# Loading, normalising and convolving in a two-layer selective-scan kernel: larger pieces of x, xn by two engines, block 3 of the convolution split between TensorE and VectorE

## The chip, the cores and the metric

The kernel runs on one core of a Trainium2 chip. The metric is device time in microseconds (us) for one launch. A difference is given against the median of several runs of the kernel before. TensorE (PE) multiplies matrices, VectorE (DVE) and ScalarE (ACT) work element by element, GpSimd (POOL) does so too, and SyncE (SP) issues most DMAs. Each engine has one queue and takes its instructions in order.

## The reference

An image of 64 x 64 positions with 96 channels passes two layers with the same skeleton. Cut to what matters here:

```python
x = x + layer0(_gn(x)); x = x + layer1(_gn(x))   # _gn: 32 groups of 3 channels, mean and variance over the image

def layer(x):                     # x: (1, 64, 64, 96), D_INNER = 192
    xz = x @ in_proj_w            # 96 -> 2 * 192
    x_val, z = split(xz)
    x_val = silu(depthwise_conv_3x3(x_val) + conv_b)
    y = sum of four selective scans of x_val over the 4096 positions
    y = layernorm(y) * silu(z)
    return y @ out_proj_w         # 192 -> 96
```

## The kernel before

Everything is fp32 and channel-major: `xT` holds 96 channels on 96 partitions by 4096 positions. The 192 inner channels are three blocks of 64, called b or T = 0, 1, 2. A block's tile has 128 partitions: the lower 64 hold the even pieces of 512 positions, the upper 64 the odd pieces, so that a tile has 4 chunks (NCH = 4) of 512 columns (HT = 512), and a chunk covers 1,024 positions.

The work runs in these stages:

- **Load** (L151 to L163). x is read in eight pieces g of 512 positions, each by one DMA, alternately from SP's and ACT's queue, into tiles `xt` with four buffers. TensorE transposes each piece in four parts into PSUM (`pt`), and VectorE copies `pt` to `xT` (L163). After that, VectorE takes the group statistics (`bn_stats`, L1268), and one DMA writes all of `xT` to a DRAM tensor `xs` (L1269), from which the end of the layer reads it again.
- **Head of a layer** (`head`, L1044 to L1180). `bn_aggr` and two small matmuls with the averaging matrix `gav` (L1064, L1070) give the group mean `gm` and, through ACT's Ln and Exp (L1071, L1072), the reciprocal deviation `rs`. VectorE normalises `xT` to `xn` in eight pieces (L1077). TensorE projects `xn` into each block: `project(b, c)`, copied by ACT into a padded image `pad[b]` (L1088), and `borders(b)`, the rows above and below each piece (L1102, copied at L1106). The depthwise 3x3 convolution then runs on two engines at once. Blocks 0 and 1 are done by VectorE in `conv(b, s)`, for two chunks at a time: one multiply (L1158) and eight multiply-adds (L1160). Block 2 is done by TensorE in `conv_by_products(2, c)`: nine matmuls per chunk with diagonal matrices `diag` that ACT makes (L1172). `finish` adds bias and Silu on ACT (L1127), giving `u`, and ACT starts `y` (L1042). Last, `gate(b, c)`, twelve times: TensorE projects `z` (L1114), ACT takes Silu into one of three buffers `sz` (L1119), and a DMA on SP's queue writes it to DRAM (L1120).
- **Scans.** Layer 0 goes through `near_scans`, which needs all of `u` and starts with matmuls `nu<-u,wide` (L276). Layer 1 goes through `scans`, a long loop whose order is pinned by hand once it has begun; it starts with a load of ACT's function table (L84) and the projections `pj<-u,xw`.
- **Tail** (`tail`): layer norm, gate, output projection, the sum with x, and for layer 0 the `bn_stats` of the next layer (L1243).

Outside the pinned loop, a planner orders each engine's queue: it goes through the instructions by priority (the order of the program text) as its own model thinks them ready, hands out buffers, and sets the waits. An instruction further down in the text can therefore stand earlier in a queue. For example, the DMA of `ipw` (L1274) stands in SP's queue at 2.21 us, before the DMA of `xs` (L1269) at 15.91 us.

The block order in the head before is:

```python
conv(0, 0)
for c in range(NCH):
    conv_by_products(2, c)
for b, s in ((1, 0), (0, 1), (1, 1)):
    conv(b, s)
```

Of the kernel before, what the change touches and what calls it, by code (L numbers as in the profile page):

```python
# [8 lines left out]
F32 = mybir.dt.float32  # L9
BF16 = mybir.dt.bfloat16  # L10
AF = mybir.ActivationFunctionType
ALU = mybir.AluOpType
# [4 lines left out]
HW = 64  # L17
L = HW * HW
DM = 96
# [5 lines left out]
HT = TC // 2  # L25
NCH = L // TC
SR = HT // HW
# [16 lines left out]
def two_ss2d_layers(  # L44
# [29 lines left out]
    nc = tc.nc  # L74

    const = ctx.enter_context(tc.tile_pool(name="const", bufs=1))
    pers = ctx.enter_context(tc.tile_pool(name="pers", bufs=1))
# [13 lines left out]
    ident = const.tile([128, 128], F32, name="ident")  # L91
# [25 lines left out]
    eps5 = const.tile([128, 1], F32, name="eps5")  # L117
    nc.vector.memset(eps5, 1e-5)
    gav = const.tile([DM, DM], F32, name="gav")
    nc.sync.dma_start(out=gav, in_=gavg)  # L120

# [23 lines left out]
    xs = dpool.tile([DM, L], F32, name="xs")  # L147
# [2 lines left out]

    xp = ExitStack()  # L151
    xT = xp.enter_context(tc.tile_pool(name="xT0", bufs=1)).tile([DM, L], F32, name="xT0")
    with tc.tile_pool(name="ld", bufs=4) as ld, tc.tile_pool(
        name="ldp", bufs=4, space=PSUM
    ) as ldp:
        xr = x.rearrange("(g j p) c -> g p j c", p=128, j=4)
        for g in range(8):
            xt = ld.tile([128, 4, DM], F32, tag="xt", name=f"xt{g}")
            (nc.sync if g % 2 == 0 else nc.scalar).dma_start(out=xt, in_=xr[g])
            pt = ldp.tile([DM, 512], F32, tag="pt", name=f"pt{g}")  # L160
            for j in range(4):
                nc.tensor.transpose(pt[:, j * 128 : (j + 1) * 128], xt[:, j, :], ident)
            nc.vector.tensor_copy(xT[:, g * 512 : (g + 1) * 512], pt)  # L163

    def columns(t, h, cols):

# [874 lines left out]
    def start_y(mul, ds, T, s=slice(0, L // 2)):  # L1041
        mul(y[T][:, s], u[T][:, s], ds[:, T : T + 1])  # L1042

    def head(l, xT, w):  # L1044

        ipw_s, v, ds = w["ipw"], w["v"], w["ds"]
        with ExitStack() as sc:
            cv = sc.enter_context(tc.tile_pool(name=f"cv{l}", bufs=1))
            cw = sc.enter_context(tc.tile_pool(name=f"cw{l}", bufs=3))
# [7 lines left out]
                nc.gpsimd.memset(t[HALF[1], NCH - 1, SR + 1, 1 : HW + 1], 0.0)  # L1057


            gst = cv.tile([DM, 6], F32, name=f"gst{l}")  # L1060
            gm, rs = gst[:, 2:3], gst[:, 5:6]
            nc.vector.bn_aggr(gst[:, 0:2], w["st"].rearrange("p a b -> p (a b)"))
            pm = cvp.tile([DM, 1], F32, tag="z", name=f"pm{l}", bufs=3)
            nc.tensor.matmul(pm, gav, gst[:, 0:1], start=True, stop=True)  # L1064
# [6 lines left out]
            nc.scalar.activation(rs, pv, AF.Ln, bias=eps5[0:DM])  # L1071
            nc.scalar.activation(rs, rs, AF.Exp, scale=-0.5)  # L1072

            xn = cv.tile([DM, L], F32, name=f"xn{l}")
            for g in range(8):
                s = slice(g * 512, (g + 1) * 512)
                nc.vector.tensor_scalar(xn[:, s], xT[:, s], gm, rs, ALU.subtract, ALU.mult)  # L1077
            xr = xn.rearrange("p (r w) -> p r w", w=HW)

            def project(b, c):  # L1080
# [43 lines left out]
            W2 = HW + 2  # L1124

            def finish(b, cut, of):
                nc.scalar.activation(  # L1127
                    u[b][:, cut].rearrange("p (c r w) -> p c r w", r=SR, w=HW), of, AF.Silu,
                    bias=v[:, b, V_CB : V_CB + 1],
                )  # L1130
                start_y(nc.scalar.mul, ds, b, cut)

            def conv_by_products(b, c):

                ps = cvp.tile([128, HT], F32, tag="in", name=f"cp{l}_{b}_{c}", bufs=3)
                for k, (i, j) in enumerate(taps):
                    nc.tensor.matmul(  # L1137
                        ps.rearrange("p (r w) -> p r w", w=HW), diag[:, k, :],
                        pad[b][:, c, i : i + SR, j : j + HW],
                        start=(k == 0), stop=(k == len(taps) - 1),  # L1140
                    )
                finish(
                    b, slice(HT * c, HT * (c + 1)), ps.rearrange("p (c r w) -> p c r w", c=1, w=HW)
                )

            def conv(b, s):


                room = cw.tile([128, 2, SR, W2], F32, tag="acc", name=f"acc{l}_{b}_{s}")
                acc = room.rearrange("p c r w -> p c (r w)")[:, :, 0 : SR * W2 - 2]  # L1150
                for k, (i, j) in enumerate(taps):
                    o = i * W2 + j
                    src = pad[b].rearrange("p c r w -> p c (r w)")[
                        :, 2 * s : 2 * s + 2, o : o + SR * W2 - 2
                    ]
                    wk = v[:, b, V_CW + k : V_CW + k + 1]
                    if k == 0:
                        nc.vector.tensor_scalar_mul(acc, src, wk)  # L1158
                    else:
                        nc.vector.scalar_tensor_tensor(acc, src, wk, acc, ALU.mult, ALU.add)  # L1160
                finish(b, slice(1024 * s, 1024 * (s + 1)), room[:, :, :, 0:HW])

            for b in (0, 1, 2):
                project(b, 0)
# [5 lines left out]
            diag = cv.tile([128, len(taps), 128], F32, name=f"diag{l}")  # L1170
            for k in range(len(taps)):
                nc.scalar.mul(diag[:, k, :], ident, v[:, 2, V_CW + k : V_CW + k + 1])  # L1172
            conv(0, 0)
            for c in range(NCH):
                conv_by_products(2, c)
            for b, s in ((1, 0), (0, 1), (1, 1)):
                conv(b, s)
            for b in range(3):
                for c in range(NCH):
                    gate(b, c)  # L1180
# [82 lines left out]
                    if 0 <= i - lag < NCH:  # L1263
                        step(order[i - lag])

    st = [pers.tile([DM, 8, 6], F32, name=f"st{l}") for l in range(2)]
    for g in range(8):
        nc.vector.bn_stats(st[0][:, g, :], xT[:, g * 512 : (g + 1) * 512])  # L1268
    nc.sync.dma_start(out=xs, in_=xT)  # L1269
    for l in range(2):  # L1270

        w = {"st": st[l], "next": st[1]}
        ipw_s = w["ipw"] = wts.tile([DM, 2 * DI], F32, name=f"ipw{l}")
        nc.sync.dma_start(out=ipw_s, in_=ipw[l])  # L1274
        v = w["v"] = wts.tile([128, 3, NV], F32, name=f"v{l}")
        op = w["op"] = wts.tile([128, 3, DM], F32, name=f"op{l}")
        for half in HALF:
            nc.sync.dma_start(out=v[half], in_=vec[l].rearrange("(b p) n -> p b n", b=3))
        for half in HALF:
            nc.sync.dma_start(out=op[half], in_=opw[l].rearrange("(b p) n -> p b n", b=3))  # L1280
        ds = w["ds"] = wts.tile([128, 3], F32, name=f"ds{l}")
        nc.vector.reduce_sum(ds, v[:, :, V_D : V_D + 4], axis=AX.X)
        sw = scan_weights(l)

        head(l, xT, w)
        xp.close()
        if l:
            scans(sw)
        else:
            covered = near_scans(sw)  # L1290
            with tc.If(covered < 1):
                for T in range(3):
                    start_y(nc.scalar.mul, ds, T)
                far_scans(sw)
        xp = ExitStack()
        xT = xp.enter_context(tc.tile_pool(name=f"xT{l + 1}", bufs=1)).tile(
            [DM, L], F32, name=f"xT{l + 1}"
        )
        tail(l, w, xT)
# [80 lines left out]
```

## Time and profile before

| what | us |
|---|---|
| median of 3 runs (1557.27 to 1559.94) | 1559.88 |
| the profiled execution | 1555.25 |
| its span, first to last instruction | 1553.5 |
| layer 0: start to first `bn_aggr` | 20.07 |
| layer 0: first `xn` to first VectorE convolution instruction | 22.89 to 31.17 |
| layer 0: convolution on VectorE | 31.17 to 73.8 |
| layer 0: convolution on TensorE | 42.19 to 73.4 |
| layer 0: first `sz` to first matmul of `near_scans` | 74.42 to 88.33 |
| layer 1: first `xn` to first VectorE convolution instruction | 224.67 to 233.61 |
| layer 1: convolution on VectorE | 233.61 to 276.24 |
| layer 1: first `sz` to table load of `scans` | 276.85 to 288.93 |

Over the whole span VectorE is busy for 87%, TensorE for 81%, ACT for 77% and GpSimd for 70%; these are means over all stages. In the profile's notation, "out<-in" names the tile written and the tiles read, and a bracket at the end of a timeline row gives the idle time before it and what released it. An fp32 matmul is carried out as two records in the trace, so `x144` matmuls of `cp` are 72 calls, 36 in each layer.

### The profile page before, as it was taken

How to read it: one execution, taken by the hardware profiler on the slowest of the kernel's cores; microseconds unless marked ns; L12 is line 12 of the kernel's file. 1: busy time of each engine (PE TensorE's matmuls, PEld its weight loads, DVE VectorE, ACT ScalarE, POOL GpSimd, SP SyncE). 2: the span in 40 equal slices, each digit the busy share in tenths (PEclk: the TensorE clock that was granted, in tenths of full speed). 3: DMA queues.
4: the chain of work that ended last, by engine and by line, in shares of the span. 5: the costliest groups of instructions: out<-in, count | busy, mean ns of one | idle time of the engine just before them, and what ended most of it. 6: DMA issues, size and time to landing. Idle time of an engine off the chain costs nothing.

```text
span 1553.5 us, 17352 instructions
## 1 busy us (share of the span) xinstructions
PE 1256.0 (81%) x5158; PEld 504.4 (32%) x5158; DVE 1350.1 (87%) x932; ACT 1203.1 (77%) x2476; POOL 1093.8 (70%) x577
## 2 busy tenths in 40 slices
PE   5954779769888979887888889797978888876778
PEld 3433424223233323332333333333333332322223
DVE  6836489339999999999999999999999999999976
ACT  3445134759999898989999999999898989987733
POOL 0032000019898989899998989898989999998750
PEclk8975689759999999999989999999999899999999
DMA  4031320432626263544526262526263443626233
GB/s 110 20 107 35 105 71 1 134 73 55 138 57 136 64 145 80 123 100 92 134 68 151 59 138 56 136 57 149 68 138 82 110 110 82 136 62 152 60 93 83
DMA packets 83059, 146.33 MB, mean 94 GB/s; under 512 B 31580, under 2 KB 33820, under 8 KB 82860
## 3 DMA queue, kind: packets, MB, share of 16 engines
q1 hardware_dynamic: 80844, 144.35, 38.4%
q10 hardware_dynamic: 2112, 0.79, 0.2%
q8 instruction: 42, 0.69, 0.2%
q14 instruction: 61, 0.50, 0.1%
HBM read 80.85 MB, written 12.13 MB: 60 GB/s over the span
## 4 chain that ended last, share of the span: by engine, by line
DVE 28%; issue 22%; PE 13%; ACT 10%; POOL 5%; DMA 5%; SPq 4%; DVEq 0%; POOLq 0%; ACTq 0%
DVE h L670 18%; DVE b L670 7%; POOL hc L670 4%; SPq L670 4%; ACT a L670 3%; PE ys L670 3%; DMA cb<-C 3%; PE b L670 2%; PE cp L1137 2%; ACT bT L670 2%; PE pj L670 2%; PE pd L670 1%; DVE w L670 1%; PE in L1084 1%; PE m L1205 1%
## 5 line engine op out<-in xcount | busy, mean ns | idle before, releaser
L670 POOL TENSOR_TENSOR hc<-h,cb 128x1024 f32<-128x1024 f32 x384 | 902.8, 2368 | 204.1 <-DMA dt<-sp 95.5
L670 DVE TENSOR_TENSOR_SCAN h<-a,carry,b 128x1024 f32<-128x1024 f32 x288 | 665.1, 2337 | 27.0 <-PE b L670 5.6
L670 ACT ACTIVATE a<-dt,am 128x1024 f32<-128x1024 f32 x384 | 438.6, 1143 | 92.3 <-DVE h L670 90.6
L670 PE MATMUL ys<-hc,fold 128*64 128x512 f32 x1536 | 429.4, 639 | 3.5 <-POOL hc L670 3.5
L670 ACT ACTIVATE bT<-duT,BT 128x192 f32<-128x192 f32 x1024 | 391.6, 445 | 5.1 <-PE b L670 3.0
L670 PE MATMUL b<-ident,bT 128*128 128x128 f32 x1536 | 222.0, 287 | 33.8 <-DVE h L670 27.6
L670 DVE TENSOR_TENSOR b<-b,du 128x1024 f32<-128x1024 f32 x192 | 232.0, 1208 | 3.5 <-PE b L670 3.2
L670 DVE TENSOR_TENSOR_SCAN h<-a,b 128x1024 f32<-128x1024 f32 x96 | 216.0, 2277 | 20.2 <-PE b L670 12.9
L670 PEld LDWEIGHTS b<-ident,bT 128*128 128x128 f32 x1536 | 174.2, 146 | 158.7 <-DVE h L670 99.7
L670 PE MATMUL b<-B,selh 96*128 96x512 bf16 x384 | 122.2, 401 | 96.1 <-DVE h L670 95.4
L670 PEld LDWEIGHTS ys<-hc,fold 128*64 128x64 f32 x1536 | 78.5, 139 | 140.8 <-issue 97.5
L670 PE MATMUL pd<-xd,dwb 29*64 29x512 f32 x192 | 60.3, 693 | 53.7 <-DVE w L670 46.9
L670 PEld LDWEIGHTS <-selh 96*128 96x128 bf16 x384 | 26.1, 98 | 222.5 <-DVE h L670 126.8
L670 PE MATMUL pj<-u,xw 64*124 64x512 f32 x192 | 94.2, 636 | 2.4 <-ACT sz L1119 1.7
L1160 DVE SCALAR_TENSOR_TENSOR acc<-pad,v,acc 128x1052 f32<-128x1052 f32 x64 | 79.6, 1308 | 0.2
L670 POOL TENSOR_TENSOR ln<-ln,w 128x512 f32<-128x512 f32 x45 | 57.6, 1279 | 14.8 <-DVE w L670 14.8
L670 PE MATMUL ys<-y,ident 128*128 128x512 f32 (+1 forms) x120 | 63.3, 634 | 0.0
L1137 PE MATMUL cp<-pad,diag 128*128 128x512 f32 x144 | 62.3, 593 | 0.0
L670 ACT CAST B<-pj 96x512 bf16<-96x512 f32 (+2 forms) x96 | 55.1, 575 | 6.4 <-PE pj L670 6.3
L670 POOL TENSOR_TENSOR sp<-sp,ln 128x512 f32<-128x512 f32 x45 | 57.5, 1278 | 0.0
L670 DVE SCALAR_TENSOR_TENSOR w<-pd,w 128x512 f32<-128x512 f32 x48 | 32.1, 668 | 29.2 <-ACT pd L670 28.6
L670 POOL TENSOR_TENSOR su<-sp,u 128x512 f32<-128x512 f32 x45 | 57.3, 1274 | 0.0
(164 smaller groups left out, 1142.2 us busy)
## 6 DMA issues: line engine op xcount, KB each, us to landing
cb<-C SPq DMA_DIRECT2D x256, 256.0 KB, 4.1
dt<-sp SPq DMA_DIRECT2D x192, 128.0 KB, 4.3
du<-su SPq DMA_DIRECT2D x192, 128.0 KB, 3.9
szd<-sz SPq DMA_DIRECT2D x24, 256.0 KB, 3.1
szt<-szd SPq DMA_DIRECT2D x24, 256.0 KB, 6.5
xT<-xs SPq DMA_DIRECT2D x8, 384.0 KB
xs<-xT SPq DMA_DIRECT2D x1, 1536.0 KB
xs<-xT SPq DMA_DIRECT2D x8, 192.0 KB, 2.3
```

The costliest lines, as they stand in the source:

```text
L670: ins = op(*args, **more)
L1084: nc.tensor.matmul(ps[half], ipw_s[:, 64 * b : 64 * b + 64], xn[:, g * 512 : (g + 1) * 512], start=True, stop=True,)
L1137: nc.tensor.matmul(ps.rearrange("p (r w) -> p r w", w=HW), diag[:, k, :], pad[b][:, c, i : i + SR, j : j + HW], start=(k == 0), stop=(k == ...
L1160: nc.vector.scalar_tensor_tensor(acc, src, wk, acc, ALU.mult, ALU.add)
L1205: nc.tensor.matmul(pm, pos, y[T][:, cut], start=(T == 0), stop=(T == 2))
```

## The change

The change has four parts.

1. x is read with four consecutive positions on each partition (1,536 consecutive bytes) in place of four rows of 384 bytes that lie 128 positions apart. There are eight buffers, all eight DMAs stand ahead of the transposes, and ACT in place of VectorE copies `pt` to `xT`, writing every fourth column. `bn_stats` reads `pt` in PSUM rather than `xT`.
2. The DMA of `xs` now directly follows the load, and the DMA of `gav` follows that of `xs`; before, `gav` was the first DMA of all.
3. The eight pieces of `xn` are split: VectorE does the even ones, ACT the odd ones, as `Identity(rs * x + shift)`, with a new small VectorE instruction for `shift = -gm * rs`.
4. `conv` takes any slice of chunks. Chunk 3 of block 2 moves from TensorE to VectorE, behind the other VectorE convolutions.

```diff
-    nc.sync.dma_start(out=gav, in_=gavg)
...
+    st = [pers.tile([DM, 8, 6], F32, name=f"st{l}") for l in range(2)]
-    with tc.tile_pool(name="ld", bufs=4) as ld, tc.tile_pool(
+    with tc.tile_pool(name="ld", bufs=8) as ld, tc.tile_pool(
         name="ldp", bufs=4, space=PSUM
     ) as ldp:
-        xr = x.rearrange("(g j p) c -> g p j c", p=128, j=4)
+        xr = x.rearrange("(g p j) c -> g p j c", p=128, j=4)
+        xts = [ld.tile([128, 4, DM], F32, tag="xt", name=f"xt{g}") for g in range(8)]
         for g in range(8):
-            xt = ld.tile([128, 4, DM], F32, tag="xt", name=f"xt{g}")
-            (nc.sync if g % 2 == 0 else nc.scalar).dma_start(out=xt, in_=xr[g])
-            pt = ldp.tile([DM, 512], F32, tag="pt", name=f"pt{g}")
+            (nc.sync if g % 2 == 0 else nc.scalar).dma_start(out=xts[g], in_=xr[g])
+        for g in range(8):
+            pt = ldp.tile([DM, 4, 128], F32, tag="pt", name=f"pt{g}")
             for j in range(4):
-                nc.tensor.transpose(pt[:, j * 128 : (j + 1) * 128], xt[:, j, :], ident)
-            nc.vector.tensor_copy(xT[:, g * 512 : (g + 1) * 512], pt)
+                nc.tensor.transpose(pt[:, j], xts[g][:, j, :], ident)
+            nc.scalar.copy(
+                xT[:, g * 512 : (g + 1) * 512].rearrange("c (p j) -> c j p", j=4), pt
+            )
+            nc.vector.bn_stats(st[0][:, g, :], pt.rearrange("c j p -> c (j p)"))
+    nc.sync.dma_start(out=xs, in_=xT)
+    nc.sync.dma_start(out=gav, in_=gavg)
...
+            nc.vector.scalar_tensor_tensor(shift, gm, -1.0, rs, ALU.mult, ALU.mult)
             xn = cv.tile([DM, L], F32, name=f"xn{l}")
             for g in range(8):
                 s = slice(g * 512, (g + 1) * 512)
-                nc.vector.tensor_scalar(xn[:, s], xT[:, s], gm, rs, ALU.subtract, ALU.mult)
+                if g % 2 == 0:
+                    nc.vector.tensor_scalar(xn[:, s], xT[:, s], gm, rs, ALU.subtract, ALU.mult)
+                else:
+                    nc.scalar.activation(xn[:, s], xT[:, s], AF.Identity, bias=shift, scale=rs)
...
             def conv(b, s):
-                room = cw.tile([128, 2, SR, W2], F32, tag="acc", name=f"acc{l}_{b}_{s}")
+                n = s.stop - s.start
+                room = cw.tile([128, 2, SR, W2], F32, tag="acc", name=f"acc{l}_{b}_{s.start}")
+                room = room[:, 0:n]
...
-                        :, 2 * s : 2 * s + 2, o : o + SR * W2 - 2
+                        :, s, o : o + SR * W2 - 2
...
-                finish(b, slice(1024 * s, 1024 * (s + 1)), room[:, :, :, 0:HW])
+                finish(b, slice(HT * s.start, HT * s.stop), room[:, :, :, 0:HW])
...
-            conv(0, 0)
-            for c in range(NCH):
+            conv(0, slice(0, 2))
+            for c in range(NCH - 1):
                 conv_by_products(2, c)
-            for b, s in ((1, 0), (0, 1), (1, 1)):
-                conv(b, s)
+            for b, c in ((1, 0), (0, 2), (1, 2)):
+                conv(b, slice(c, c + 2))
+            conv(2, slice(NCH - 1, NCH))
...
-    st = [pers.tile([DM, 8, 6], F32, name=f"st{l}") for l in range(2)]
-    for g in range(8):
-        nc.vector.bn_stats(st[0][:, g, :], xT[:, g * 512 : (g + 1) * 512])
-    nc.sync.dma_start(out=xs, in_=xT)
```

More of the change, by code (lines that the diff above doesn't have):

```diff
@@ L1057, in head @@
                 nc.gpsimd.memset(t[HALF[1], NCH - 1, SR + 1, 1 : HW + 1], 0.0)
-            gst = cv.tile([DM, 6], F32, name=f"gst{l}")
-            gm, rs = gst[:, 2:3], gst[:, 5:6]
+            gst = cv.tile([DM, 7], F32, name=f"gst{l}")
+            gm, rs, shift = gst[:, 2:3], gst[:, 5:6], gst[:, 6:7]
             nc.vector.bn_aggr(gst[:, 0:2], w["st"].rearrange("p a b -> p (a b)"))
```

## The prediction

> **What bounds the kernel now.** I read the page, then the chain of waits from 0 to 330 us, then the timeline of the three stretches that the change touches: the load (0 to 23 us) and the heads of layer 0 (23 to 88 us) and layer 1 (222 to 289 us). The rest, some 1,380 us of scans and tails, has no edited line; I take it as a constant that starts earlier or later. The chain's groups by line, in that window, put the convolution on TensorE first:
>
> ```profile
> by line: PE cp L1137 9.4%; PE in L1084 4.5%; issue 3.8%; PE pj L670 3.1%; PE m L1205 2.2%; DMA szd<-sz 1.5%; DVE g L1226 1.3%; ACT bT L670 1.2%; ACT sz L1119 1.2%; DVE y L1207 1.1%; DVE g L1223 0.9%; PE pd L670 0.9%; ACT diag L1172 0.8%; DV
> ...
> 244.71 31.10 PE cp L1137 x72
> ...
> 282.10 2.46 DMA szd<-sz
> ```
>
> So in a head the chain goes through the 72 records of `cp`, then the gates. The timeline of the load and of layer 0's head, and VectorE's of layer 1:
>
> ```profile
> 6.55 0.17 DVE L1282 TENSOR_REDUCE ds<-v 128x3 f32<-128x12 f32 x1 [3.60 <-DMA v<-in_vec_dram]
> ...
> 11.62 3.53 PE L162 MATMUL pt<-ident,xt 128*96 128x128 f32 x16 [3.48 <-DMA xt<-in_x_dram]
> ...
> 15.80 4.24 DVE L1268 BATCH_NORM_STATS2 st<-xT 96x6 f32<-96x512 f32 x7
> ...
> 20.07 0.37 DVE L1062 BATCH_NORM_AGGREGATE gst<-st 96x2 f32<-96x48 f32 x1
> ...
> 71.12 2.67 DVE L1160 SCALAR_TENSOR_TENSOR acc<-pad,v,acc 128x1052 f32<-128x1052 f32 x2
> ...
> 73.29 5.47 PE L1114 MATMUL z<-xn,ipw 96*64 96x512 f32 x24
> ...
> 74.42 0.60 ACT L1119 ACTIVATE sz<-z 128x512 f32<-128x512 f32 x1 [0.33 <-PE z L1114]
> ...
> 76.00 1.15 ACT L1127 ACTIVATE u<-acc,v 128x1024 f32<-128x1024 f32 x1
> ...
> 88.33 0.59 PE L276 MATMUL nu<-u,wide 128*128 128x192 f32 x2 [1.64 <-ACT sz L1119]
> ...
> 258.75 17.49 DVE L1160 SCALAR_TENSOR_TENSOR acc<-pad,v,acc 128x1052 f32<-128x1052 f32 x14
> ```
>
> The reader is to see three things. The second half of the transposes waits 3.48 us for a load that SP issues only at 8.70. VectorE then does seven `bn_stats` when all transposes are over. And in both heads VectorE (last convolution instruction ends 73.8 and 276.2) and TensorE (73.4 and 275.8) finish together, after which VectorE idles while twelve gates take 12 to 14 us.
>
> **What the Trainium skill says.** "VectorE: DVE Perf Modes", section on the perf-mode tier table: fp32 single-source operations in SBUF run at twice the rate, two-source ones at once. The trace agrees: 0.76 us for the multiply of L1158, 1.31 us for the multiply-add of L1160, both 1,052 wide. "ScalarE: Activation LUTs", section on what ACT_TABLE_LOAD costs: each pointer operand adds about 93 ns to an ACTIVATE; the trace has 0.59 us for a 512-wide copy and 0.69 us with a bias pointer, so two pointers are at most 0.8 us. "DMA: Bandwidth & Descriptors", section on issuing engines: DMAs from any engine interleave on the same 16 DMA engines; here these ran at 303 to 341 GB/s from 3 to 5 us, whichever queue issued. "TensorE: Matmul & The Clock Gate", Part 1: the clock halves after an idle window of some 3.4 us; the trace shows 0.50 from 12 to 14 us and from 20 to 26 us. I expect the projections to meet the half clock as before.
>
> **Load.** All eight DMAs are issued within about 3 us: four per queue at 0.4 to 0.5 us. 1.5 MB at 310 GB/s is 5 us, done near 7.3 us, and the wait at 11.59 goes. TensorE then needs 32 x 0.226 = 7.2 us from 4.5: end at 11.7. ACT's copies (0.59 us each, against 0.9 us of transposes per piece) hide beside TensorE; strided writes of ACT have no row here, and I bound them at 0.59 to 1.2 us; at 1.2 the last copy ends near 15. `bn_stats` (0.6 us apart) hides too if VectorE is free: then `bn_aggr` comes at 12.5, 7.6 us earlier. It may not be free: `ds<-v` blocked VectorE's queue until 6.55, with 2.7 us of constants behind it. SP now issues two more x loads ahead of `v`, which I estimate to land near 8.3, and eight `bn_stats` after the constants end at 8.3 + 0.2 + 2.6 + 4.8 = 15.9: 4.2 us earlier. I cannot see the new queue; I take 5.8, between the two. Bounds 4.2 and 7.6.
>
> **gav and xs.** `gav` now stands behind `xs` in the text. `xs` waits for all of `xT` (near 12.5), and its 1.5 MB takes 5 us. If the queue followed the text, `gav` would come near 20 and hold `pm` (20.6 before): the load's gain would be 0.5. But SP's queue before holds `ipw`, `v`, `op` and `xw` ahead of `xs`, though they stand behind it in the text, as they need no wait. I cost this at nothing, and keep the other as a rival.
>
> **xn.** Eight pieces 0.455 us apart took 3.73. Now `shift` costs 0.19 (the row of the other 96x1 operations), then four pieces per engine take 1.9 to 2.6. ACT has a gap there (its first `pad` copy waited 3.09 us). So the last `xn` comes about 1.1 us earlier, but TensorE's projections at half clock are nearly as slow as `xn` was: in layer 0 the eight records of `in` take 23.48 to 26.95 at any rate. I take a start of the convolution 0.1 us earlier in layer 0 and 0.6 us in layer 1 (first `ed` there at 230.21, against 228.9 for TensorE alone). Bounds: -0.2 to 1.2 each.
>
> **Convolution.** Let S be VectorE's first convolution instruction. TensorE loses 18 of 72 records of 0.433 us (31.2/72): 7.8 us. `cp` started at S + 11.0 and will end at S + 34.4 instead of S + 42.2. VectorE gains one multiply and eight multiply-adds, 526 wide. From 1.31 us at 1,052 and about 0.74 us at 512 (the `g<-y,v,rstd` rows), one takes 0.76 us, or 0.68 us apart when interleaved; the sum is 0.4 + 8 x 0.68 to 8 x 0.81 = 5.8 to 6.9 us. I take 6.2: VectorE ends at S + 42.6 + 6.2 = S + 48.8. ACT's `u` and `y` add 0.74 + 0.62.
>
> The gates can now run beside VectorE. They needed 15.0 us after `cp` in layer 0 (73.3 to 88.3) and 13.1 in layer 1: they end at S + 49.4 and S + 47.5. In layer 0 the next matmuls start with T = 0 and reach T = 2 only 5 us later (88.33, 93.41), so the gates decide: S + 49.5 against S + 57.2, a gain of 7.7, of which I take 7.5. In layer 1 VectorE and ACT decide, since the last Silu must precede the table load: S + 50.2 against S + 55.3 (288.93 - 233.61), a gain of 5.1. Bounds per head: 4.0 to 8.
>
> **Sum.** 5.8 + 0.1 + 7.5 + 0.6 + 5.1 = 19.1 us. The profiled execution, 1555.25, becomes 1536.2. The median shown is 4.6 above that execution; the same gain gives 1559.88 - 19.1 = 1540.8, and I predict 1541.
>
> **Rivals.**
> 1. The load gives nearly nothing, since `gav` or a wait of `bn_stats` behind `ds` keeps `bn_aggr` near 20: 19.1 - 5.3 = 13.8 gained, 1546. For it: the order of the text, and VectorE's 3.60 us wait for `v`. Against it: SP's queue before.
> 2. VectorE becomes the bound in both heads and loses more: last chain not overlapped (6.9 us), spread behind late ACT steps; or the gates' DMAs, each buffer `sz` waiting for its write, spread over a longer time. Heads gain 3 each, load 4.2: 10 gained, 1550. For it: VectorE had no slack, 42.49 us busy in 31 to 74. Against it: the gates' 12 us cover it.
> 3. Slower: the planner puts the gates' Silus behind `u` of the new last convolution, as in the text. ACT works in order, so twelve gates, less the three that PSUM holds ready, start at S + 49.5 and end at S + 63.5 (layer 0) and S + 61.6: 6.3 us later per head, 12.6 in all, against 6.5 from the load and `xn`: 1566. It decides from about half the gates being held in both heads. Against it: before, `sz` at 74.42 stands ahead of `u<-acc` at 76.00 in ACT's queue, though behind it in the text.
>
> **Chances and range.** Forecast 0.70, first rival 0.14, second 0.08, slower rival 0.05, and 0.03 for a shift in the scans that eats half the gain or more. A measurement can tell about 0.2%, 3.1 us. The range takes in the load's bounds (1.6 down, 1.8 up), the convolution's, both smaller rivals in part, and 3 us of measuring: 1533 to 1551. Faster by over 0.2%: 0.91; within: 0.03; slower: 0.06.
>
> **What would show it.** Right: no DMA wait inside the transposes; `bn_aggr` between 12 and 16 us; 54 `cp` records per head; `sz` rows among `acc` rows; `nu` at 88.33 less 13.4, near 75; the table load of `scans` at 288.93 less 19, near 270. Wrong: `gav` late and `pm` waiting for it; `bn_stats` behind `ds`; ACT waiting for `acc` with `z` ready; or a main loop of another length than before.

## The result and the profile after

The changed kernel takes 1613.18 us (median of 4 runs, 1610.28 to 1614.73) against 1558.58 us before (4 runs): a ratio of 1.0339, 95% interval 1.0302 to 1.0376. That is about 55 us slower, where 19 us faster was forecast, and far outside the range. Both heads did become shorter. What grew is the part of the program that no line of the change touches.

The page of the changed kernel, its chain of waits and one row of its costliest groups (the columns of the row are line, engine, operation and count, then busy us and mean ns, then idle time before):

```profile
span 1612.3 us, 17407 instructions
...
PE 1285.4 (80%) x5122; PEld 511.1 (32%) x5122; DVE 1359.8 (84%) x936; ACT 1338.1 (83%) x2590; POOL 1095.4 (68%) x577
...
ACT 37%; DVE 19%; issue 14%; PE 13%; DMA 3%; SPq 3%; POOL 0%; DVEq 0%; ACTq 0%
ACT a L677 11%; DVE h L677 10%; ACT bT L677 9%; ACT L677 6%; DVE b L677 4%; PE pj L677 4%; PE ys L677 3%; SPq L677 3%; DMA cb<-C 3%; PE b L677 2%; DVE acc L1174 2%; ACT ln L677 2%; ACT pd L677 1%; ACT B L677 1%; PE m L1220 1%
...
L677 ACT ACT_TABLE_LOAD x97 | 124.5, 1283 | 1.4
```

The page of the kernel before, in the same places:

```profile
PE 1256.0 (81%) x5158; PEld 504.4 (32%) x5158; DVE 1350.1 (87%) x932; ACT 1203.1 (77%) x2476; POOL 1093.8 (70%) x577
...
DVE 28%; issue 22%; PE 13%; ACT 10%; POOL 5%; DMA 5%; SPq 4%; DVEq 0%; POOLq 0%; ACTq 0%
```

Read the busy times first. ACT has 135 us more work, no other engine more than 30, and ACT's share of the chain rises from 10% to 37%. One row explains 124.5 of the 135: 97 loads of ACT's function table in the scans, 1.283 us each. Most of the rest is the work that the change gives to ACT, the copies of `pt` and half of `xn`. The kernel before has no load there; it has one for the scans, ahead of them. L677 is the helper through which the scans record their instructions. "ACT L677 6%" in the chain names no tile, as the loads do not, so I take it to stand for them.

Where they begin is seen in ACT's timeline at the end of layer 1's head. In the kernel before, the last Silu of the convolution (`u<-acc`) stands well ahead of the load:

```profile
278.43 1.15 ACT L1127 ACTIVATE u<-acc,v 128x1024 f32<-128x1024 f32 x1
...
287.59 1.32 ACT L1119 ACTIVATE sz<-z 128x512 f32<-128x512 f32 x2 [0.26 <-DMA szd<-sz]
288.93 1.28 ACT L84 ACT_TABLE_LOAD   x1
```

In the changed kernel it does not; the last line here is VectorE's:

```profile
268.78 1.16 ACT L1049 ACTIVATE y<-u,ds 128x1024 f32<-128x1024 f32 x1
269.82 0.61 ACT L1131 ACTIVATE sz<-z 128x512 f32<-128x512 f32 x1
270.44 1.28 ACT L84 ACT_TABLE_LOAD   x1
271.74 1.03 ACT L233 ACTIVATE am<-ab 64x48 f32<-64x48 f32 x4
272.78 1.28 ACT L1139 ACT_TABLE_LOAD   x1
274.08 0.72 ACT L1139 ACTIVATE u<-acc,v 128x512 f32<-128x512 f32 x1
...
272.90 0.76 DVE L1174 SCALAR_TENSOR_TENSOR acc<-pad,v,acc 128x526 f32<-128x526 f32 x1
```

The explicit load of the table that holds both Exp and Ln (L84) comes at 270.44, right behind the last gate. The Silu of the new last convolution, `u<-acc` at 274.08, is still to come, because VectorE ends that convolution only at 273.7. So its own table is loaded at 272.78, and the common table is gone. From then on the program loads one table for each Exp that follows an Ln and one for each Ln that follows an Exp. ACT's timeline inside the scans, later:

```profile
568.30 1.28 ACT L677 ACT_TABLE_LOAD   x1
569.60 0.72 ACT L677 ACTIVATE ln<-w,one 128x512 f32<-128x512 f32 x1
570.23 0.67 ACT L677 ACTIVATE pd<-w,one 128x512 f32<-128x512 f32 x1
570.84 0.44 ACT L677 ACTIVATE bT<-duT,BT 128x192 f32<-128x192 f32 x1
571.30 1.28 ACT L677 ACT_TABLE_LOAD   x1
572.59 1.15 ACT L677 ACTIVATE a<-dt,am 128x1024 f32<-128x1024 f32 x1
```

The kernel before runs the same instructions with no load among them:

```profile
563.22 0.72 ACT L670 ACTIVATE ln<-w,one 128x512 f32<-128x512 f32 x1
563.84 0.68 ACT L670 ACTIVATE pd<-w,one 128x512 f32<-128x512 f32 x1
564.46 0.44 ACT L670 ACTIVATE bT<-duT,BT 128x192 f32<-128x192 f32 x1
564.80 1.14 ACT L670 ACTIVATE a<-dt,am 128x1024 f32<-128x1024 f32 x1
```

There are 48 such Ln (three blocks in each of 16 groups), two loads for each: 96 of the 97. The other stands ahead of the first Exp, at 285.86. "ScalarE: Activation LUTs" of the Trainium skill, section on table sets, describes both halves: a set is loaded where the active one lacks the function, and `natural_log_exp_and_others` holds Exp and Ln at once. The trace agrees on the first half. It also shows that having a set that holds both is no guarantee that it is the one loaded.

What a stage costs is seen in the windows of both kernels (columns: window, length, then busy us with count for TensorE, its weight loads, VectorE, ACT and GpSimd, the clock, DMA share and GB/s), first before:

```profile
500.00:600.00 100.00, 85.53 (x375) 32.28 (x375) 96.47 (x55) 88.59 (x180) 94.34 (x49) 0.97 0.37 91
```

and then after:

```profile
500.00:600.00 100.00, 84.66 (x348) 31.68 (x348) 89.67 (x50) 97.00 (x186) 88.43 (x45) 0.91 0.36 85
```

In the scans ACT goes from 89 to 97 of 100 us and VectorE from 96 to 90: the limit has moved from VectorE to ACT. TensorE's granted clock is lower as well, 0.886 in the mean over the span against 0.910, and its busy time is 29 us longer with 36 records fewer. How much of the loss comes directly from ACT's time and how much by way of that clock, these runs do not separate.

The account closes at ACT's first copy of `xd`, where the scans begin to work. It comes at 291.88 before and at 277.00 after, 14.9 us earlier. From there to the end it is 1553.5 - 291.88 = 1261.6 us before and 1612.3 - 277.00 = 1335.3 us after, 73.7 longer. The difference, 58.8 us, is that of the spans.

### The profile page after: what moved, and what is told of

The parts are those of the page before. It is cut to its first block, busy times and chain, and to the rows that moved or that the text cites. A ratio compares the mean times of both kernels' runs of the same rounds, so it can differ in the third digit from the quotient of the medians.

```text
span 1612.3 us, 17407 instructions
## 1 busy us (share of the span) xinstructions
PE 1285.4 (80%) x5122; PEld 511.1 (32%) x5122; DVE 1359.8 (84%) x936; ACT 1338.1 (83%) x2590; POOL 1095.4 (68%) x577
## 4 chain that ended last, share of the span: by engine, by line
ACT 37%; DVE 19%; issue 14%; PE 13%; DMA 3%; SPq 3%; POOL 0%; DVEq 0%; ACTq 0%
ACT a L677 11%; DVE h L677 10%; ACT bT L677 9%; ACT L677 6%; DVE b L677 4%; PE pj L677 4%; PE ys L677 3%; SPq L677 3%; DMA cb<-C 3%; PE b L677 2%; DVE acc L1174 2%; ACT ln L677 2%; ACT pd L677 1%; ACT B L677 1%; PE m L1220 1%
## 5 line engine op out<-in xcount | busy, mean ns | idle before, releaser
L677 POOL TENSOR_TENSOR hc<-h,cb 128x1024 f32<-128x1024 f32 x384 | 903.3, 2365 | 269.3 <-DVE h L677 109.4
L677 DVE TENSOR_TENSOR_SCAN h<-a,carry,b 128x1024 f32<-128x1024 f32 x288 | 665.6, 2338 | 41.4 <-PE b L677 12.9
L677 ACT ACTIVATE a<-dt,am 128x1024 f32<-128x1024 f32 x384 | 438.1, 1141 | 56.2 <-DVE h L677 54.3
L677 PE MATMUL ys<-hc,fold 128*64 128x512 f32 x1536 | 441.9, 656 | 3.5 <-POOL hc L677 3.5
L677 ACT ACTIVATE bT<-duT,BT 128x192 f32<-128x192 f32 x1024 | 390.8, 445 | 2.1
L677 PE MATMUL b<-ident,bT 128*128 128x128 f32 x1536 | 234.3, 293 | 66.8 <-ACT bT L677 35.0
L677 DVE TENSOR_TENSOR b<-b,du 128x1024 f32<-128x1024 f32 x192 | 232.7, 1212 | 32.3 <-PE b L677 31.9
L677 PEld LDWEIGHTS b<-ident,bT 128*128 128x128 f32 x1536 | 181.0, 148 | 206.9 <-DVE h L677 96.0
L677 DVE TENSOR_TENSOR_SCAN h<-a,b 128x1024 f32<-128x1024 f32 x96 | 216.6, 2279 | 27.0 <-PE b L677 20.4
L677 PE MATMUL b<-B,selh 96*128 96x512 bf16 x384 | 126.2, 412 | 89.4 <-DVE h L677 87.7
L677 ACT ACT_TABLE_LOAD x97 | 124.5, 1283 | 1.4
L677 PEld LDWEIGHTS ys<-hc,fold 128*64 128x64 f32 x1536 | 79.6, 141 | 144.2 <-issue 107.3
L677 PE MATMUL pj<-u,xw 64*124 64x512 f32 x192 | 101.3, 686 | 8.8 <-ACT sz L1131 3.5
L677 PE MATMUL pd<-xd,dwb 29*64 29x512 f32 x192 | 66.4, 756 | 41.3 <-DVE w L677 34.3
L677 PEld LDWEIGHTS <-selh 96*128 96x128 bf16 x384 | 26.7, 100 | 225.7 <-DVE h L677 116.7
L1174 DVE SCALAR_TENSOR_TENSOR acc<-pad,v,acc 128x1052 f32<-128x1052 f32 (+1 forms) x80 | 91.3, 1198 | 0.6
L677 DVE SCALAR_TENSOR_TENSOR w<-pd,w 128x512 f32<-128x512 f32 x48 | 32.4, 674 | 46.6 <-ACT pd L677 44.6
L677 POOL TENSOR_TENSOR ln<-ln,w 128x512 f32<-128x512 f32 x45 | 57.3, 1274 | 16.2 <-DVE w L677 16.2
L677 PE MATMUL ys<-y,ident 128*128 128x512 f32 (+1 forms) x120 | 66.9, 667 | 0.0
L677 ACT CAST B<-pj 96x512 bf16<-96x512 f32 (+2 forms) x96 | 55.2, 576 | 5.8 <-PE pj L677 5.8
L1224 ACT ACTIVATE sq<-y 128x512 f32<-128x512 f32 x24 | 14.5, 627 | 52.6 <-DMA xT<-xs 31.4
L677 PEld LDWEIGHTS pj<-u,xw 64*124 64x124 f32 x192 | 35.2, 202 | 70.4 <-issue 40.7
```

Source lines behind the costliest of these rows:

```text
L677: ins = op(*args, **more)
L1224: nc.scalar.activation(sq, y[T][:, cut], AF.Square)
```

## The experiments

Theory: the loss is the 97 table loads, and they come only from the place of the one explicit load, ahead of the last Silu. Rivals: the work given to VectorE and ACT in the heads disturbs the scans by itself; or the load or the split `xn` does.

**1. The last convolution traced behind the gates.**

```diff
-            conv(2, slice(NCH - 1, NCH))
             for b in range(3):
                 for c in range(NCH):
                     gate(b, c)
+            conv(2, slice(NCH - 1, NCH))
```

> The changed kernel with the last convolution (block 2, chunk 3) traced behind the gates instead of ahead of them, so that the one table load of the scans, which is pinned behind the last ACT instruction traced, comes after the last Silu. Theory (table loads): 1 load in the scans in place of 97, the scans' part as long as before (about 1262 us from the first copy of xd to the end instead of 1335), and the heads' gain stays: 1538 to 1544 us. Rival (the work given to VectorE and ACT in the heads upsets the scans whatever the tables): above 1590 us.

Measured: 1544.1 us, ratio to before 0.989, interval 0.9862 to 0.9918. ACT's timeline of this kernel at the same place:

```profile
268.94 0.61 ACT L1131 ACTIVATE sz<-z 128x512 f32<-128x512 f32 x1
271.33 0.72 ACT L1139 ACTIVATE u<-acc,v 128x512 f32<-128x512 f32 x1 [1.78 <-DVE acc L1174]
272.08 0.72 ACT L1049 ACTIVATE y<-u,ds 128x512 f32<-128x512 f32 x1
272.81 1.28 ACT L84 ACT_TABLE_LOAD   x1
```

The load now comes behind the Silu and the start of `y` that follows it, 2.4 us later than in the changed kernel, and there is not one load in the scans. The same arithmetic, with one line moved, is some 69 us faster than the changed kernel and faster than before. The rival falls. The median lies just above the upper edge of what was expected (1538 to 1544); the profiled execution took 1540.90.

**2. Parts 1 to 3 alone.** Block 2 of the convolution (the third, called block 3 in the title) is wholly on TensorE again.

```diff
-            for c in range(NCH - 1):
+            for c in range(NCH):
                 conv_by_products(2, c)
...
-            conv(2, slice(NCH - 1, NCH))
```

> The changed kernel with block 2 of the convolution wholly on TensorE again: load, gav, and split xn stay. Theory (table loads): the last Silu before the gates is again early, 1 load in the scans; the load gives about 2 us, the split xn takes 0.7 to 1.1 back in each head: 1556 to 1559 us. Rival (the load or the split xn brings the loss): above 1590 us.

Measured: 1559.79 us, ratio 0.9982, interval 0.9963 to 1.0001. No table load stands in the scans. The larger loads, ACT's copies and the split `xn` bring neither the loss nor a gain that can be told from none (1556 to 1559 us was expected): the first copy of `xd` comes at 291.70 against 291.88 before. So the gain of the first experiment is the convolution's.

**3. The loads alone, in the kernel before.** The explicit table load of the scans is left out; nothing else is changed.

```diff
-            load_exp_ln()
             am = decays(weights[2])
             carry = pre.tile([128, 3, NP], F32, name="carry")
```

> The kernel before without the explicit table load at the start of the scans, nothing else. Theory (table loads): Exp and Ln then get a set each, about 96 loads of 1.28 us in the scans, 123 us of ACT, and the time rises by about 70 to 78 us, to 1629 to 1637 us. Rival (loads hide in ACT's idle time, 77% busy before): within 15 us of before, 1558 to 1573 us.

Measured: 1628.83 us, ratio 1.0404, interval 1.0348 to 1.046, at the lower edge of what was expected. The groups of this kernel by line and form:

```profile
L670 ACT ACT_TABLE_LOAD x96 | 123.2, 1283 | 1.4
```

Without any of the four parts, the kernel before gets 96 loads in its scans; from the first copy of `xd` to the end it takes 1630.5 - 295.49 = 1335.0 us, the same as the changed kernel's 1335.3. The loads suffice for the whole loss. The rival, that they hide in ACT's idle time, falls.

**4. Half of the loads.** The changed kernel with a second explicit load of the common table ahead of group 8 of 16.

```diff
                 steps = []
+                if k == 8:
+                    steps += [(-13.5, load_exp_ln)]
```

> The changed kernel with one more explicit load of the common table ahead of group 8 of 16 in the scans. Theory (table loads): about 49 of the 97 loads go, and half of the 74 us with them: 1573 to 1580 us. Rival (something else makes every group longer): 1608 to 1615 us.

Measured: 1584.25 us, ratio 1.0131, interval 1.0079 to 1.0182. Its groups by form:

```profile
L677 ACT ACT_TABLE_LOAD x49 | 62.9, 1283 | 0.7
```

Within one kernel the groups change where the loads stop. The table is worked out from the first copy of `xd` of each group (mean us between those of neighbouring groups, from group 3 on):

| kernel | groups 3 to 8 | groups 9 to 15 |
|---|---|---|
| before | 72.6 | 72.7 |
| changed | 77.2 | 77.0 |
| experiment 1 | 72.3 | 73.0 |
| experiment 4 | 78.0 | 72.9 |

The other kernels without loads (experiments 2, 5, 6 and 7) lie between 73.0 and 74.8 in both columns. Six loads of 1.283 us are 7.7 us per group, of which between 2 and 5 show; the rest presumably goes into gaps that ACT had. The time fell by 29 us and not by the expected 33 to 40. The first groups lose more than their share: up to the first copy of group 3, the changed kernel takes 453.82 - 277.00 = 176.8 us and the kernel before 451.62 - 291.88 = 159.7, 17 of the 74 us, and experiment 4 keeps those. Not all of the 17 is the loads': experiments 1, 2, 5, 6 and 7, which have none, take 159.8 to 167.1 up to there.

**5. xn on VectorE alone**, on the kernel of the first experiment.

```diff
-                if g % 2 == 0:
-                    nc.vector.tensor_scalar(xn[:, s], xT[:, s], gm, rs, ALU.subtract, ALU.mult)
-                else:
-                    nc.scalar.activation(xn[:, s], xT[:, s], AF.Identity, bias=shift, scale=rs)
+                nc.vector.tensor_scalar(xn[:, s], xT[:, s], gm, rs, ALU.subtract, ALU.mult)
```

> The kernel of the first experiment (last convolution behind the gates) with all eight pieces of xn on VectorE again and no shift. Theory (ACT's 0.72 us per piece and the shift are slower than VectorE's 0.46, and the new order puts four more projections ahead of the borders): from the first xn to the first convolution instruction 8.3 and 8.9 us as before, not 9.6 and 9.4, so 1 to 2 us faster in all than the first experiment. Rival (the split xn gains, as the prediction had it): 1 us slower or more.

Measured: 1545.93 us, ratio 0.9925, interval 0.9899 to 0.9952. Against the first experiment's 0.989 this decides nothing: the expected gain is not seen, and the rival is not excluded. From the first `xn` to the first convolution instruction it took 8.48 and 9.81 us here, 9.61 and 9.37 with the split, 8.28 and 8.94 before. In layer 1 the projections begin while TensorE's granted clock is at 0.50, and by the shares in windows of 2 us it steps to 1.00 near 219.0 us in the first experiment and near 220.3 here, 5.9 and 7.1 us after the first `xn`; so that 9.37 and 9.81 can't be compared. In layer 0 the clock's column shows no such step in either. Whether the split helps or harms by a microsecond was not settled.

**6. The load's hidden wait removed**, on the kernel of the first experiment: `ds`, which waits for `v`, is pinned behind the `bn_stats` in VectorE's queue.

```diff
-        nc.vector.reduce_sum(ds, v[:, :, V_D : V_D + 4], axis=AX.X)
+        tc.keep_in_program_order(
+            nc.vector.reduce_sum(ds, v[:, :, V_D : V_D + 4], axis=AX.X)
+        )
```

> The kernel of the first experiment with the reduction ds, which waits for v, pinned behind the bn_stats in VectorE's queue. Theory (ds and the constants behind it hold bn_stats up, and TensorE by the four buffers of pt): the transposes run through, bn_aggr of layer 0 at 13 to 14 us instead of 18.5, and 4 to 5 us faster than the first experiment. Rival (the load is bound by ACT's strided copies, which share a bank of PSUM with bn_stats): bn_aggr at 16 us or later, less than 2.5 us faster.

Measured: 1538.85 us, ratio 0.986, interval 0.9814 to 0.9907, the lowest median of all. The load in the timeline of the changed kernel (the first experiment has it the same, `bn_aggr` at 18.49):

```profile
8.98 0.17 DVE L1293 TENSOR_REDUCE ds<-v 128x3 f32<-128x12 f32 x1 [6.03 <-DMA v<-in_vec_dram]
...
11.72 2.48 DVE L168 BATCH_NORM_STATS2 st<-pt 96x6 f32<-96x512 f32 x4
...
12.46 3.53 PE L164 MATMUL pt<-ident,xt 128*96 128x128 f32 x16 [3.90 <-DVE st L168]
...
17.41 0.69 DVE L168 BATCH_NORM_STATS2 st<-pt 96x6 f32<-96x512 f32 x1 [0.21 <-ACT xT L165]
...
18.14 0.37 DVE L1069 BATCH_NORM_AGGREGATE gst<-st 96x2 f32<-96x48 f32 x1
```

and in that of this experiment:

```profile
6.13 0.69 DVE L168 BATCH_NORM_STATS2 st<-pt 96x6 f32<-96x512 f32 x1 [0.39 <-ACT xT L165]
...
6.46 3.69 PE L164 MATMUL pt<-ident,xt 128*96 128x128 f32 x20 [0.62 <-DMA xt<-in_x_dram]
...
13.23 0.69 DVE L168 BATCH_NORM_STATS2 st<-pt 96x6 f32<-96x512 f32 x1 [0.20 <-ACT xT L165]
...
13.96 0.37 DVE L1069 BATCH_NORM_AGGREGATE gst<-st 96x2 f32<-96x48 f32 x1
```

VectorE no longer stands 6.03 us for `v`, TensorE no longer stands 3.90 us for VectorE to free `pt`, and `bn_aggr` comes 4.5 us earlier than in experiment 1. The gain lasts to the end of layer 1's head: the first copy of `xd` comes at 270.42, against 275.15. In the time it is not settled. The ratios 0.986 and 0.989 are 0.3% apart, some 5 us, which fits, but their intervals overlap; of the 5.3 us between the medians 3.4 also lie between the medians of the kernel before that stood beside them (1557.83 and 1561.26).

**7. Both edits.**

> Both edits on the kernel of the first experiment. If the two add up: 5 to 7 us faster than it, 1535 to 1539 us, the fastest of all kernels here. If the load's gain is taken back by a later wait in layer 0: no better than the better of the two alone.

Measured: 1543.77 us, ratio 0.9886, interval 0.9839 to 0.9932. The two don't add up in the time: this is no better than experiment 6, and the intervals overlap. In the traces, too, the heads are not shorter: the first copy of `xd` comes at 273.10, against 270.42 in experiment 6. At the first copy of the next group it is ahead (306.31 against 308.02), and from there to the end it takes longer (1549.1 - 306.31 = 1242.8 against 1236.4). The length of the scans varies by some 10 us between executions, with the granted clock (0.914 in the profiled execution of experiment 1, 0.904 to 0.901 in those of 5 to 7), so that a difference of 2 us in a head can't be told from these times.

## Why the prediction was wrong

**The step that failed** stands in the paragraph on the convolution: "In layer 1 VectorE and ACT decide, since the last Silu must precede the table load". Nothing in the program made it precede. The explicit load is held behind the ACT instruction traced last before it, the `sz` of the last gate, and behind nothing else. Before, the last `u<-acc` ended at 279.58 and the load began at 288.93, so the order was right with 9 us to spare, without being guaranteed. The change delays the last Silu by the new convolution and brings the gates forward, and the order turns over. The prediction's own figures hold this: it has the gates of layer 1 end at S + 47.5 and the Silu after them, at S + 50.2. The load came at S + 47.2 (270.44 - 223.28), with the gates. In place of a load behind the last Silu stand 97 loads in the scans, 124.5 us of ACT's time, and a main part 73.7 us longer. Experiment 1 restores the order with one moved line, and the loss is gone.

**From this followed the second failure**, the sentence that the rest "has no edited line; I take it as a constant". ACT's table is a state that outlives the head. No rival had it; "a shift in the scans that eats half the gain or more" had a chance of 0.03, without a mechanism. The slower rival saw the planner's freedom to reorder gates and Silus but put the harm in the other direction, gates behind the Silu. The trace shows gates ahead of it, as that rival's own counter-evidence said, and I didn't ask what else was ordered only by the gates. The last thing that "what would show it" names, a main loop of another length, is what happened.

**The load** was sized at 5.8 us with bounds 4.2 and 7.6; `bn_aggr` came at 18.14, 1.9 earlier: outside the bounds, and near to the first rival, which named a wait of `bn_stats` behind `ds`. The wait for `v` was named and its landing (8.3 predicted, 8.98 measured as the start of `ds`) was nearly right. What I left out: with `bn_stats` reading `pt`, four buffers stop TensorE until VectorE is free (3.90 us, of which experiment 6 leaves 0.19), and each `bn_stats` of the second half follows ACT's copy of its own piece, some 0.9 us apart where I had 0.6. ACT's strided copy, 1.09 us in the mean, is inside the bounds of 0.59 to 1.2. `gav` was issued at 1.20, ahead of `xs` at 17.43, as costed. The reading of 303 to 341 GB/s from 3 to 5 us was off at its lower end: the windows show 308 and 341, and 303 stands at 18 to 20 us.

**xn** was to gain 0.1 and 0.6. The start of the convolution came 8.95 and 10.07 us after the first `xn` in the changed kernel, against 8.28 and 8.94: no gain. Four pieces in a row take ACT 2.93 us at 21.00, some 0.72 apart, within the bound of 0.8 each. The sign stays open, as experiment 5 says.

**The convolution** was right in its mechanism and in most of its terms, and its gain came out larger than predicted. VectorE's ends 48.9 us after its start in layer 0 (78.73 - 29.84; predicted 48.8). TensorE in layer 0 of the changed kernel:

```profile
38.75 23.45 PE L1149 MATMUL cp<-pad,diag 128*128 128x512 f32 x54
...
76.78 0.66 PE L283 MATMUL nu<-u,wide 128*128 128x192 f32 x2 [3.49 <-ACT sz L1131]
```

The 54 records take the 23.4 us that were worked out, and the first `nu` follows their end by 14.6 us, where 15.0 was taken. But `cp` starts at S + 8.9 (so it does in experiment 2) and not at S + 11.0, so `nu` comes at S + 46.9 and not at S + 49.5. In experiment 1 the table load of layer 1 comes at S + 50.4 (272.81 - 222.40; predicted 50.2). The first copy of `xd` comes at 275.15 in experiment 1 and at 291.70 in experiment 2, so the split is worth 16.5 us against 12.6 predicted.

**The sum.** Without the lost table, experiment 1 is 1.1% faster, 17 us of 1561, interval 13 to 22; 19.1 was predicted. That these are so close is luck in part: in experiment 1 the load gave 1.6 us of its 5.8 (`bn_aggr` at 18.49), the stretch from `xn` to the convolution grew by 1.8 us in the two heads together where 0.7 less was expected, and the convolution gave some 4 us more than its 12.6. What turned a gain into a loss is the state that the edits left behind, which did not enter the sum.

## What to carry to other kernels

When a change makes one instruction later or another earlier, list what is ordered only by habit: an ACT function table, and any load that is pinned to a neighbour and not to the instruction it must follow. Count the table loads in a program before and after an edit; one Silu behind the load cost 97 loads, and it cost them in a loop that the edit doesn't touch. Where a function set matters for a long loop, set it again at the loop's start, behind everything that could change it.

## What the runs showed of the hardware

- A table load in the scans holds ACT for 1.28 us. The one at 568.30 begins within 0.02 us of the end of the instruction before it (567.72 + 0.56), and the next instruction starts within 0.02 us of its own end (568.30 + 1.28, next at 569.60). "ScalarE: Activation LUTs" of the Trainium skill, section on what ACT_TABLE_LOAD costs, adds some 1.38 us of drain to each switch; no such time is seen here.
- ACT's copy from PSUM with every fourth column written took 1.09 us in the mean for 96x512 (eight in the changed kernel), against 0.59 for the 128x512 copy into rows of 64.
- `bn_stats` of a piece begins only when ACT's copy of the same `pt` is over (idle of 0.20 us, released by `ACT xT`), though both only read it. What imposes that order was not tried apart.
- TensorE stood 3.49 us ahead of `pj` in experiment 1, waiting for the last gate, and the granted clock fell to 0.50 there (0.52 from 270 to 275 us, against 0.98 to 1.00 in the kernel before while it runs `pj`): the twelve records of `pj` took 8.05 us against 3.80. In the kernel before the clock fell to 0.50 too, but later (295 to 300 us), so that the wait is not shown to be what brings it down.
